# Two graph layers on one core: complex products added up in PSUM in the first batch, block sums of graph 56 and the order of graph 63

## Chip, cores, metric

One Trainium2 chip, one of its cores. The metric is the device time of one execution in microseconds (us); the time of a kernel is the median of its runs. The engines are called PE (TensorE), DVE (VectorE), ACT (ScalarE), POOL (GpSimd) and SP (SyncE, which here only issues transfers).

## What is computed

Input are 64 graphs of N = 256 nodes with D = 256 features, `x` (64, 256, 256), and their adjacency matrices `adj` (64, 256, 256), all in float32. Two layers follow each other; BN is a batch normalisation with given statistics, LN a normalisation over the features without weights.

```
# layer 0
h      = relu(BN1(conv1x1(x)))                       # over the nodes, D channels
x_conv = relu(BN2(conv17(h)) + x)
s      = x @ w_se.T + b_se                           # 3 features
A      = exp(-|s_i - s_j|^2) * adj
msg    = relu(x @ w_msg.T + b_msg)
x_nmp  = A @ msg
x1     = LN(x + GRUcell([x_conv, x_nmp], x))         # gates r, z, n
# layer 1
h      = LN(x1) * gamma + beta
conv   = (adj @ h) @ W_rel + b_rel + h @ W_root
out    = LN(x1 + (x1 + relu(conv)))
```

## The kernel before

**Batches.** The graphs are worked in 8 batches of 8. The convolution with 17 taps is computed for a whole batch in a transform domain: the features of the batch are folded and split by a tree of DVE steps over slots of one large tile, `XF` (also seen as `X`, with 256 columns to a slot), into 15 leaves, most of them complex pairs. Each complex leaf is multiplied by its filter with three real products, k1 = (sum slot) x w0, re x w1 and im x w2. `products` (L387) takes two leaves at a time: it writes the three products into three PSUM banks by `product` (L384, matmuls at L385), and its inner function `take` copies k1 to SBUF on ACT (L400) and writes k1 - p3 (DVE, L401) and k1 + p2 (DVE, L402) back into the slots. Seven such pairs and `last_products` make up the 15 leaves. The merges of the way back are DVE steps at L303 and L305 (each on the real and imaginary slots together), then `stt` (L104). At the end `second` and `third` write the slots that PE transposes back and adds to the transposed x (`turned_x`, L539, and L574, tile `ps_xc`); ACT takes the result through a relu into `xc` (L579).

**The first batch.** The convolution of batch 0 runs alone, ahead of the loop, with filters that are made on the way and lie in one tile (`w2all`, in the pool `first_pool`). Between its pairs of leaves (counted in `count`) stand steps for the first graphs: messages of graph 0 after the third pair and of graph 1 after the fourth (`messages`, L639, on PE, ACT and POOL), then factors and distances of graph 0, and after the leaf products messages of graph 2. `first_pool.close()` then lets `adj`, `wih` and `x` be loaded into the space.

**The loop.** For every graph the loop of a batch issues the gates of the GRU cell (`gates_rz`, L713 and L715, and `gates_n`, L725 and L727), the step `update` (new x and h), the transposes of h and the projection of the graph before (L869, L882), its aggregation (L894, tile `y`), and the message passing of graphs ahead. `pump` inserts steps of the next batch's convolution between them. `STAGE` says how far a convolution is; `pump` reads it to start preparations for the last batch.

**The last batch.** Graphs 56 to 62 compute their gates with seven block products in place of eight (`block_gates`, L774, tiles `ps_a` to `ps_d`, matmuls at L786, DVE's `onto` at L791). The left factors are blocks of x, nmp and xc and four sums of such blocks, which `block_sums(k, i)` makes with four DVE steps per input (L768 to L771). The second pair of products, in ps_b and ps_c, reads the sums of all three inputs. Graph 56's sums are made by `pump` in the loop of batch 6, once its inputs exist (`early_sums`, L1148); those of 57 to 62 are made in the turn of the graph before.

**The last graph.** `last_graph` (L919) works graph 63 in two halves of 128 nodes. `half(n)` is a generator with steps that the body calls by `step`: nn with a tanh; w, its statistics and POOL's power chain `scales` (L932, L933); h (L957) and the shift (POOL, L938 and L939); x1 (ACT, L960). Around them stand, in the order written out by hand, the gates, `project(62)`, `aggregate(62)`, the transposes of h (`turn_half`, L966) and the projections (`project_half`, L974) of each half, the sums over the neighbours (L1003) and the last normalisation. For n = 0 that is a shift on POOL and an activation on ACT (L1015), for n = 1 a DVE step (L1017); each half has its own output transfer.

**What sets the order.** Every engine runs its instructions in program order and waits at the first that isn't ready. PSUM has eight banks of one tag, handed out in turn by `bank`; a bank is reused when the readers of its last content are through.

Of the kernel before, what the change touches and what calls it, by code (L numbers as in the profile page):

```python
# [13 lines left out]
AF = mybir.ActivationFunctionType  # L14
ALU = mybir.AluOpType

P = 128
B, N, D = 64, 256, 256
C = D // P
# [10 lines left out]
BG = 8  # L30
NB = B // BG
# [16 lines left out]
LEAVES = [(V + k, V + 8 + k, a) for k, a in enumerate(leaf_angles(PI / 2, 8))]  # L48
# [28 lines left out]
def gnn_two_layers(  # L77
# [17 lines left out]
    nc = tc.nc  # L95
# [4 lines left out]
    def bank(name):  # L100
        return psum.tile([P, 512], F32, tag="ps", name=name)
# [143 lines left out]
    def sl(a, n, step=1):  # L245
        return X[:, a:a + n] if step == 1 else X[:, a:a + (n - 1) * step + 1:step]
# [133 lines left out]
        nc.sync.dma_start(out=t[:, :n], in_=w2m[first:first + n].rearrange("f c p o -> p f c o"))  # L380
        return lambda m, c: t[:, m, c, :]

    def product(ps, slot, w, m):
        for c in range(C):  # L384
            nc.tensor.matmul(ps, X[:, slot, c * P:(c + 1) * P], w(m, c), start=(c == 0), stop=(c == C - 1))  # L385

    def products(b, first, sums):  # L387

        p1, p2, p3 = bank("ps_k1"), bank("ps_k2"), bank("ps_k3")
        re, im, _ = LEAVES[first]  # L390
        for k in range(2):
            w = load_w(b, 3 * (first + k), 3)
            at = slice(k * D, (k + 1) * D)
            product(p1[:, at], sums + k, w, 0)
            product(p2[:, at], re + k, w, 1)
            product(p3[:, at], im + k, w, 2)

        def take():
            k1 = sl(sums, 2).rearrange("p s e -> p (s e)")
            nc.scalar.copy(k1, p1)  # L400
            nc.vector.tensor_sub(sl(re, 2).rearrange("p s e -> p (s e)"), k1, p3)  # L401
            nc.vector.tensor_add(sl(im, 2).rearrange("p s e -> p (s e)"), k1, p2)  # L402
        return take

    def last_products(b):
# [29 lines left out]
    def conv(b):  # L435
# [150 lines left out]
            yield from second(j)  # L586
        for j in range(8):
            yield from third(j)
        STAGE[b] = "out"

        def channels(q):
            for o in range(C):
# [128 lines left out]
    def gates_n(k, n):  # L721
        q, ins = inputs(k, n)
        pn = bank("ps_n")
        for c in range(C):
            nc.tensor.matmul(pn[:, D:], XT[k][:, c, q], whh[:, c, 2 * D:], start=(c == 0), stop=(c == C - 1))  # L725
        for i, t in enumerate(ins):
            nc.tensor.matmul(pn[:, :D], t, wih[:, i, 2 * D:], start=(i == 0), stop=(i == 3))  # L727
        nc.vector.tensor_add(RZ[k][1][:, n, :], pn, brzn[:, 2 * D:])  # L728
# [186 lines left out]
    def step(g):  # L915
        if g is not None:
            next(g, None)


    def last_graph(y_before, k):  # L920
        nn, w, y = (work.tile([P, C, D], F32, tag=t, name=t, bufs=b) for t, b in (("nn", 1), ("w", 1), ("y", 2)))
        H[k] = work.tile([P, C, D], F32, tag="h", name="h", bufs=1)
        X1[k] = work.tile([P, C, D], F32, tag="x1", name="x1", bufs=2)

        hT, hr = (XF[:, i * C * D:(i + 1) * C * D].rearrange("p (c n) -> p c n", c=C) for i in range(2))
        outs = []

        def scales(mv, columns):

            q = work.tile([P, 2], F32, tag="q", name="qh", bufs=4)  # L930
            for i, (f, e) in enumerate(columns):
                nc.gpsimd.tensor_scalar(q[:, i:i + 1], mv[:, 1:2], f, e, ALU.mult, ALU.add)  # L932
            nc.gpsimd.tensor_tensor(q[:, :len(columns)], q[:, :len(columns)], mhalf[:, :len(columns)], ALU.pow)  # L933
            return q

        def shift(mv, q):
            sh = work.tile([P, 1], F32, tag="sh", name="shh", bufs=4)
            nc.gpsimd.tensor_mul(sh, mv[:, 0:1], q[:, 0:1])  # L938
            nc.gpsimd.tensor_scalar(sh, sh, -1.0, None, ALU.mult)  # L939
            return sh  # L940

        def half(n):
            rz, gn = RZ[k]
            a, c = nn[:, n, :], w[:, n, :]
            stt(a, rz[:, n, :D], 1.0, gn[:, n, D:], op0=ALU.add, op1=ALU.mult)
            stt(a, a, 0.5, gn[:, n, :D])
            nc.scalar.activation(a, a, AF.Tanh)
            yield
            nc.vector.tensor_sub(c, XG[k][:, n, :], a)
            stt(c, rz[:, n, D:], 3.0, c, op0=ALU.add, op1=ALU.mult)  # L950
            stt(c, a, 4.0, c)
            mv = work.tile([P, 1, 2], F32, tag="mv", name="mvh", bufs=4)
            stats(mv, 0, c)
            mv = mv[:, 0, :]
            q = scales(mv, [(1.0, 4 * EPS), (1 + EPS, 4 * EPS * EPS)])
            yield
            nc.vector.tensor_scalar(H[k][:, n, :], c, mv[:, 0:1], q[:, 1:2], ALU.subtract, ALU.mult)  # L957
            sh = shift(mv, q)
            yield
            nc.scalar.activation(X1[k][:, n, :], c, AF.Identity, bias=sh, scale=q[:, 0:1])  # L960
            yield

        def turn_half(n):
            ps = bank("ps_hT")
            for c in range(C):
                nc.tensor.transpose(ps[:, c * P:(c + 1) * P], H[k][:, n, c * P:(c + 1) * P], ident)  # L966
            for c in range(C):
                nc.scalar.activation(hT[:, c, n * P:(n + 1) * P], ps[:, c * P:(c + 1) * P], AF.Identity,
                                     bias=gb[:, 1, c:c + 1], scale=gb[:, 0, c:c + 1])

        def project_half(n):
            ps = bank("ps_out")
            for c in range(C):
                nc.tensor.matmul(ps, hT[:, c, n * P:(n + 1) * P], wrr[:, c, :], start=(c == 0), stop=(c == C - 1))  # L974
            nc.scalar.copy(hr[:, n, :], ps[:, :D])
            outs.append(ps)

        halves_ = [half(n) for n in range(C)]
        gates_rz(k, 0)
        gates_n(k, 0)  # L980
        step(y_before)
        transposes_h(k - 1)
        step(halves_[0])
        gates_rz(k, 1)
        step(halves_[0])
        gates_n(k, 1)
        step(halves_[1])
        step(halves_[0])
        step(halves_[0])
        project(k - 1)  # L990
        step(halves_[1])
        turn_half(0)
        step(halves_[1])
        agg = aggregate(k - 1)
        step(agg)
        turn_half(1)
        step(halves_[1])
        project_half(0)
        project_half(1)
        step(agg)  # L1000
        for m in range(C):
            for n in range(C):
                nc.tensor.matmul(outs[n][:, D:], ADJ[k][:, m, n * P:(n + 1) * P], hr[:, m, :], start=False,  # L1003
                                 stop=(m == C - 1), skip_group_check=True)
        step(agg)
        for n in range(C):
            o = y[:, n, :]
            nc.vector.tensor_add(o, outs[n][:, D:], brel)
            stt(o, o, 0.0, X1[k][:, n, :], op0=ALU.max, op1=ALU.add)
            mv = work.tile([P, 1, 2], F32, tag="mv3", name="mvy", bufs=4)  # L1010
            stats(mv, 0, o)
            q = scales(mv[:, 0, :], [(1.0, EPS / 4)])
            if n == 0:
                sh = shift(mv[:, 0, :], q)
                nc.scalar.activation(o, o, AF.Identity, bias=sh, scale=q[:, 0:1])  # L1015
            else:
                nc.vector.tensor_scalar(o, o, mv[:, 0, 0:1], q[:, 0:1], ALU.subtract, ALU.mult)  # L1017
            (nc.sync, nc.scalar)[n].dma_start(out=out[k, n * P:(n + 1) * P, :], in_=o)


# [78 lines left out]
    while STAGE.get(0) != "inverse":  # L1099
        if next(first) is None:  # L1100
            count += 1
            if count == 3:
                messages(0, True)
            elif count == 4:
                messages(1, True)
            elif count == 5:
                factors(0)
            elif count == 6:
                distances(0)
    messages(2, True)  # L1110
    first_pool.close()

# [16 lines left out]
    POINTS = 10  # L1129
    y_left = None  # L1130
    sums_left = weight_blocks()
    early_sums = [0, 1, 2]
    for b in range(NB):
        coming = conv(b + 1) if b + 1 < NB else iter(())
        done, at, goal = 0.0, 0, BG * POINTS - 6
# [1 line left out]
        def pump():  # L1137
            nonlocal done, at
            at += 1
            while done < CONV_WEIGHT * at / goal:  # L1140
                t = next(coming, 1e9)
                if t is None:
                    break
                done += t
            if STAGE.get(NB - 1) in ("inverse", "out"):
                next(sums_left, None)

            if STAGE.get(NB - 1) == "out" and (NB - 1) * BG in NMP and len(early_sums) > (done < 1e8):  # L1148
                block_sums((NB - 1) * BG, early_sums.pop(0))

        if b == NB - 1:
            break
# [44 lines left out]
    for _ in sums_left:  # L1197
        pass
    first_k = (NB - 1) * BG
    for i in early_sums:  # L1200
        block_sums(first_k, i)
    for k in range(first_k, B - 1):
        load(k + 3)
# [74 lines left out]
```

## Time and profile before

| what | us |
|---|---|
| median of five runs | 2257.08 |
| lowest, highest | 2253.61, 2258.67 |
| profiled execution | 2253.61 |
| its span, first to last instruction | 2251.8 |
| TensorE's granted clock, mean over the span | 0.998 |

In the lines that follow, L12 is line 12 of the kernel before. PE is a matmul, PEld its weight load, SPq, ACTq and the like an engine's queue. A line of the chain of waits has its start, its length, engine, output tile, line and how many instructions. A line of the timeline has start, length, engine, line, operation, output and inputs, shape, and in brackets the idle time of the engine just before it with what ended it. A line of the windows has for each engine the busy time and number of instructions, then the granted clock of TensorE (1.00 is full), the busy share of the transfer engines and GB/s.

### The profile page before, as it was taken

How to read it: one execution, taken by the hardware profiler on the slowest of the kernel's cores; microseconds unless marked ns; L12 is line 12 of the kernel's file. 1: busy time of each engine (PE TensorE's matmuls, PEld its weight loads, DVE VectorE, ACT ScalarE, POOL GpSimd, SP SyncE). 2: the span in 40 equal slices, each digit the busy share in tenths (PEclk: the TensorE clock that was granted, in tenths of full speed). 3: DMA queues.
4: the chain of work that ended last, by engine and by line, in shares of the span. 5: the costliest groups of instructions: out<-in, count | busy, mean ns of one | idle time of the engine just before them, and what ended most of it. 6: DMA issues, size and time to landing. Idle time of an engine off the chain costs nothing.

```text
span 2251.8 us, 24641 instructions
## 1 busy us (share of the span) xinstructions
PE 2206.0 (98%) x8400; PEld 1463.6 (65%) x8400; DVE 1720.8 (76%) x3329; ACT 767.0 (34%) x1587; POOL 471.5 (21%) x933
## 2 busy tenths in 40 slices
PE   8999999999999999999999999999999999999998
PEld 5775666667666666656766566665666666666665
DVE  6976889388892988749987498865979478896675
ACT  6433223432235322443224432244222432224333
POOL 0101212221221221213212231221212222212212
PEclk9999999999999999999999999999999999999999
DMA  5932432214423143231522334222332314321110
GB/s 148 317 108 69 137 108 93 98 48 140 136 75 103 38 151 120 75 106 65 167 75 75 103 110 140 82 81 79 131 122 75 113 52 140 116 84 49 42 33 20
DMA packets 212682, 226.69 MB, mean 101 GB/s; under 512 B 22103, under 2 KB 203854, under 8 KB 212558
## 3 DMA queue, kind: packets, MB, share of 16 engines
q1 hardware_dynamic: 190128, 191.27, 26.4%
q10 hardware_dynamic: 22430, 33.86, 4.3%
q8 instruction: 67, 1.10, 0.2%
q14 instruction: 57, 0.47, 0.1%
HBM read 179.22 MB, written 45.88 MB: 100 GB/s over the span
## 4 chain that ended last, share of the span: by engine, by line
PE 80%; DVE 15%; issue 2%; POOL 1%; DMA 1%; ACT 1%; ACTq 0%; SPq 0%; POOLq 0%; DVEq 0%
PE ps_rz L715 16%; PE ps_k L385 10%; PE ps_rz L713 8%; PE ps_n L727 8%; PE ps_out L882 7%; DVE XF L104 5%; PE ps_c L466 5%; PE ps_nmp L697 5%; PE ps_msg L647 4%; PE ps_out L894 4%; PE ps_n L725 4%; DVE w L104 1%; DVE XF L362 1%; PE ps_dist L685 1%; DVE bst L824 1%
## 5 line engine op out<-in xcount | busy, mean ns | idle before, releaser
L104 DVE SCALAR_TENSOR_TENSOR XF<-XF 128x512 f32<-128x512 f32 (+2 forms) x800 | 507.7, 665 | 7.4
L846 POOL TENSOR_SCALAR q<-mv 128x2 f32<-128x2 f32 x63 | 31.9, 506 | 1441.1 <-DVE mv L825 1441.1
L385 PE MATMUL ps_k<-w,XF 128*128 128x256 f32 x1316 | 298.3, 382 | 14.2 <-ACT AT L687 11.6
L385 PEld LDWEIGHTS ps_k<-w,XF 128*128 128x128 f32 x1316 | 246.8, 190 | 60.6 <-ACT AT L687 17.3
L728 DVE TENSOR_TENSOR gn<-ps_n,brzn 128x512 f32<-128x512 f32 x114 | 78.3, 687 | 197.7 <-PE ps_n L727 197.7
L719 ACT ACTIVATE rz<-rz 128x512 f32<-128x512 f32 x114 | 71.8, 630 | 462.4 <-DVE rz L718 462.4
L882 PE MATMUL ps_out<-wrr,hT 128*128 128x512 f32 x504 | 226.6, 592 | 0.0
L713 PE MATMUL ps_rz<-whh,xT 128*128 128x512 f32 x456 | 214.6, 593 | 0.0
L715 PE MATMUL ps_rz<-wih,nmp 128*128 128x512 f32 x456 | 214.4, 592 | 0.0
L715 PE MATMUL ps_rz<-wih,xc 128*128 128x512 f32 x456 | 214.4, 592 | 0.0
L718 DVE TENSOR_TENSOR rz<-ps_rz,brzn 128x512 f32<-128x512 f32 x114 | 77.7, 681 | 153.4 <-PE ps_rz L715 153.3
L882 PEld LDWEIGHTS ps_out<-wrr,hT 128*128 128x128 f32 x504 | 96.0, 190 | 96.0 <-issue 84.3
L715 PEld LDWEIGHTS ps_rz<-wih,xc 128*128 128x128 f32 x456 | 86.9, 190 | 108.8 <-issue 108.6
L715 PEld LDWEIGHTS ps_rz<-wih,nmp 128*128 128x128 f32 x456 | 86.9, 190 | 108.8 <-issue 108.8
L658 ACT ACTIVATE msg<-msg 128x512 f32<-128x512 f32 x61 | 38.4, 630 | 337.9 <-DVE msg L656 337.9
L647 PE MATMUL ps_msg<-wms,xT 128*128 128x260 f32 x512 | 132.1, 396 | 4.9 <-DVE XF L401 4.9
L362 DVE TENSOR_TENSOR XF<-XF 128x512 f32<-128x512 f32 (+3 forms) x128 | 125.4, 1004 | 1.7
L466 PE MATMUL ps_c<-xTc,w 128*128 128x512 f32 x256 | 116.1, 597 | 7.0 <-ACT xTc L458 7.0
L697 PE MATMUL ps_nmp<-AT,msg 128*128 128x256 f32 x512 | 121.1, 380 | 0.0
L713 PEld LDWEIGHTS ps_rz<-whh,xT 128*128 128x128 f32 x456 | 82.3, 191 | 57.6 <-issue 54.4
L894 PE MATMUL ps_out<-hr,adj 128*128 128x256 f32 x504 | 119.6, 380 | 0.0
L883 ACT COPY hr<-ps_out 128x256 f32<-128x256 f32 x126 | 46.7, 372 | 211.1 <-PE ps_out L882 211.1
(197 smaller groups left out, 3790.0 us busy)
## 6 DMA issues: line engine op xcount, KB each, us to landing
w<-w2m SPq DMA_DIRECT2D x105, 768.0 KB, 5.9
xn<-in_x_dram SPq DMA_DIRECT2D x32, 512.0 KB, 4.4
xt<-xTc ACTq DMA_DIRECT2D x32, 512.0 KB, 3.2
xT<-xt SPq DMA_DIRECT2D x64, 256.0 KB, 2.9
xb<-in_x_dram SPq DMA_DIRECT2D x32, 512.0 KB, 5.8
adj<-in_adjT_dram SPq DMA_DIRECT2D x64, 256.0 KB, 2.7
x<-in_x_dram SPq DMA_DIRECT2D x64, 256.0 KB, 3.0
out_dram<-y ACTq DMA_DIRECT2D x63, 256.0 KB, 2.2
```

Of the source, the lines that this page charges most:

```text
L104: nc.vector.scalar_tensor_tensor(o, in0, s, in1, op0=op0, op1=op1)
L362: (nc.vector.tensor_add if add else nc.vector.tensor_sub)(sl(o, n), sl(a, n), sl(b, n))
L385: nc.tensor.matmul(ps, X[:, slot, c * P:(c + 1) * P], w(m, c), start=(c == 0), stop=(c == C - 1))
L466: nc.tensor.matmul(pss[o], w1[:, c, o * P:(o + 1) * P], xTc[:, c, :], start=(c == 0), stop=(c == C - 1))
L647: nc.tensor.matmul(ps[:, :D + 4], XT[k][:, c, m * P:(m + 1) * P], wms[:, c, :], start=(c == 0), stop=(c == C - 1 and not idle))
L697: nc.tensor.matmul(ps[:, d * N:(d + 1) * N], MSG[k][:, m, d * P:(d + 1) * P], AT[k][:, m, :], start=(m == 0), stop=(m == C - 1))
L713: nc.tensor.matmul(prz, XT[k][:, c, q], whh[:, c, 0:2 * D], start=(c == 0), stop=False)
L715: nc.tensor.matmul(prz, t, wih[:, i, 0:2 * D], start=False, stop=(i == 3))
L725: nc.tensor.matmul(pn[:, D:], XT[k][:, c, q], whh[:, c, 2 * D:], start=(c == 0), stop=(c == C - 1))
L727: nc.tensor.matmul(pn[:, :D], t, wih[:, i, 2 * D:], start=(i == 0), stop=(i == 3))
L882: nc.tensor.matmul(ps, hT[:, c, n * P:(n + 1) * P], wrr[:, c, :], start=(c == 0), stop=(c == C - 1))
L894: nc.tensor.matmul(po, ADJ[k][:, m, n * P:(n + 1) * P], hr[:, m, :], start=False, stop=(m == C - 1), skip_group_check=True)
```

## The change

Five things are changed.

- In batch 0, `products_added` takes the place of `products`. It uses two banks for a pair. PE first writes k1 into the first bank, ACT copies it to the sum slot; then PE writes im x w2 into the second bank and adds re x w1 onto k1 in the first. `take` copies that sum to the imaginary slots on ACT, and DVE has only the subtraction left.
- The messages of graph 1 move from behind the fourth pair of leaves to behind all leaf products, just ahead of those of graph 2.
- The sums of graph 56 are made at the head of the last batch and no longer in the loop of batch 6; the mark "out" goes.
- In graph 63, statistics and h of a half become one step (a `yield` goes), and the steps, transposes, projections and the aggregation stand in another order.
- The last normalisation of half 1 is done as that of half 0, by POOL and ACT.

```diff
-    def product(ps, slot, w, m):
+    def product(ps, slot, w, m, first=True):
         for c in range(C):
-            nc.tensor.matmul(ps, X[:, slot, c * P:(c + 1) * P], w(m, c), start=(c == 0), stop=(c == C - 1))
+            nc.tensor.matmul(ps, X[:, slot, c * P:(c + 1) * P], w(m, c), start=first and c == 0, stop=(c == C - 1),
+                             skip_group_check=True)
...
     def products(b, first, sums):
+        if b == 0:
+            return products_added(first, sums)
...
+    def products_added(first, sums):
+        p1, p3 = bank("ps_k1"), bank("ps_k3")
+        re, im, _ = LEAVES[first]
+        w = [load_w(0, 3 * (first + k), 3) for k in range(2)]
+        at = [slice(k * D, (k + 1) * D) for k in range(2)]
+        k1 = sl(sums, 2).rearrange("p s e -> p (s e)")
+        for k in range(2):
+            product(p1[:, at[k]], sums + k, w[k], 0, k == 0)
+        nc.scalar.copy(k1, p1)
+        for k in range(2):
+            product(p3[:, at[k]], im + k, w[k], 2)
+        for k in range(2):
+            product(p1[:, at[k]], re + k, w[k], 1, False)
+        def take():
+            nc.scalar.copy(sl(im, 2).rearrange("p s e -> p (s e)"), p1)
+            nc.vector.tensor_sub(sl(re, 2).rearrange("p s e -> p (s e)"), k1, p3)
+        return take
...
-        STAGE[b] = "out"
...
             q = scales(mv, [(1.0, 4 * EPS), (1 + EPS, 4 * EPS * EPS)])
-            yield
             nc.vector.tensor_scalar(H[k][:, n, :], c, mv[:, 0:1], q[:, 1:2], ALU.subtract, ALU.mult)
             sh = shift(mv, q)
             yield
...
         step(halves_[0])
+        step(halves_[0])
         gates_n(k, 1)
         step(halves_[1])
-        step(halves_[0])
-        step(halves_[0])
+        turn_half(0)
         project(k - 1)
+        project_half(0)
         step(halves_[1])
-        turn_half(0)
-        step(halves_[1])
+        turn_half(1)
         agg = aggregate(k - 1)
         step(agg)
-        turn_half(1)
+        project_half(1)
         step(halves_[1])
-        project_half(0)
-        project_half(1)
         step(agg)
...
             q = scales(mv[:, 0, :], [(1.0, EPS / 4)])
-            if n == 0:
-                sh = shift(mv[:, 0, :], q)
-                nc.scalar.activation(o, o, AF.Identity, bias=sh, scale=q[:, 0:1])
-            else:
-                nc.vector.tensor_scalar(o, o, mv[:, 0, 0:1], q[:, 0:1], ALU.subtract, ALU.mult)
+            sh = shift(mv[:, 0, :], q)
+            nc.scalar.activation(o, o, AF.Identity, bias=sh, scale=q[:, 0:1])
...
-            elif count == 4:
-                messages(1, True)
...
+    messages(1, True)
     messages(2, True)
     first_pool.close()
...
-    early_sums = [0, 1, 2]
...
-            if STAGE.get(NB - 1) in ("inverse", "out"):
+            if STAGE.get(NB - 1) == "inverse":
                 next(sums_left, None)
-            if STAGE.get(NB - 1) == "out" and (NB - 1) * BG in NMP and len(early_sums) > (done < 1e8):
-                block_sums((NB - 1) * BG, early_sums.pop(0))
...
-    for i in early_sums:
+    for i in range(3):
         block_sums(first_k, i)
```

## The prediction

> **What bounds the kernel now.** The first page view, busy time by engine, and the fourth, the chain that ended last, say that TensorE is the bound for most of the span:
>
> ```profile
> PE 2206.0 (98%) x8400; PEld 1463.6 (65%) x8400; DVE 1720.8 (76%) x3329; ACT 767.0 (34%) x1587; POOL 471.5 (21%) x933
> PE 80%; DVE 15%; issue 2%; POOL 1%; DMA 1%; ACT 1%; ACTq 0%; SPq 0%; POOLq 0%; DVEq 0%
> ```
>
> The 15% on DVE decide this case, because the change sits at the places where PE stops leading. There are three: the first batch (DVE leads from 105 us on), the gates of graph 56, and graph 63. I read the chain in each, then the timeline with its releasers. First the chain around the first batch (start, us, what):
>
> ```profile
> 100.14 5.39 PE ps_k L385 x24
> ...
> 105.63 0.69 DVE XF L401
> 106.31 0.61 DVE XF L402
> ...
> 106.94 0.70 DVE XF L303
> ...
> 144.75 5.24 PE ps_xc L574 x30
> 149.99 1.79 PE ps_xc L539 x16
> 151.78 3.57 PE ps_xc L574 x32
> ```
>
> DVE takes the chain over from PE at the fourth pair and gives it back 39 us later at L574. Its sub, add and merges run without a gap. 30 records of L574 first cost 5.24 us and then 32 cost 3.57. The timeline and the windows (sums, TensorE clock, DMA share) say why:
>
> ```profile
> 144.15 5.84 PE L574 MATMUL ps_xc<-ident,XF 128*128 128x128 f32 x32 [3.41 <-DVE XF L104]
> ...
> 146.00:147.00 1.00, 1.00 (x6) 1.00 (x6) 0.97 (x3) 1.00 (x2) 0.00 (x0) 0.50 0.10 33
> 149.00:150.00 1.00, 1.00 (x11) 1.00 (x11) 1.00 (x3) 0.87 (x2) 0.00 (x0) 1.00 0.00 0
> ```
>
> PE idled 3.41 us for DVE, and then worked at clock 0.50 until about 149. Now the end of the span: the chain through the gates of graph 56, and lines of the timeline there and in graph 63.
>
> ```profile
> 2054.15 1.72 PE ps_d L786 x6
> 2055.87 1.72 PE ps_b L786 x6
> 2057.59 1.72 PE ps_c L786 x6
> ```
> ```profile
> 2057.99 0.53 DVE L791 TENSOR_TENSOR XF<-ps_a,brzn 128x384 f32<-128x384 f32 x1
> ...
> 2232.49 0.18 DVE L825 BATCH_NORM_AGGREGATE mvh<-bst 128x2 f32<-128x6 f32 x1
> 2232.64 0.69 DVE L728 TENSOR_TENSOR gn<-ps_n,brzn 128x512 f32<-128x512 f32 x1
> ...
> 2238.20 0.41 DVE L957 TENSOR_SCALAR h<-w,mvh,qh 128x256 f32<-128x256 f32 x1 [1.37 <-POOL qh L933]
> ...
> 2248.55 0.41 DVE L1017 TENSOR_SCALAR y<-y,mvy,qh 128x256 f32<-128x256 f32 x1 [1.30 <-POOL qh L933]
> ```
>
> PE runs through the gates without a gap (each piece begins where the last ended). In graph 63 an h waits for POOL's power chain, and the last DVE step too.
>
> **First batch: products added in PSUM.** Per pair, one DVE add (L402) goes and one 128x512 ACT copy comes; TensorE runs the same matmuls, the four of "re" now second into the first bank. On DVE, sub to merge takes 106.94 - 105.63 = 1.31 us now. Without the add the merge follows the sub directly, 0.72 (as L303 to L305 stand now), so 0.59 per pair. Pairs 1 to 3 give nothing: DVE waits for PE at the fourth anyway (idle 103.4 to 105.63). Pairs 4 to 7 give 4 x 0.59 = 2.36. The ACT copy (group mean 579 ns) has to end before the merge as well: PE ends at 105.53, ACT can be done near 106.2, the merge is due at 106.35; for pairs 5 to 7 PE is many us ahead of DVE. The added wait on PE, that the second use of the bank comes after ACT's copy of k1, is covered: the copy ends 0.83 after its four matmuls, PE has the 1.73 us of "im" to run first, 0.9 us to spare. Without that cover it would be 0.83 a pair on the four pairs that PE leads, 3.3 us.
>
> Graph 1's messages (4 x 260-wide matmuls and two short ones per half, 3.31 us of PE at 105.35) move behind the leaf products. PE's total up to the end of nmp at 140.73 stays, so PE is free at the same time. Behind them now stand messages of graph 2 and the transposes; their banks come free by DVE subs that end 3 us or more before PE gets there. Their four ACT copies and five POOL steps move to idle engines. The pool of the first filters closes 3.3 us earlier, so SP issues adj, wih and x earlier (129.86 now); its order is the same.
>
> DVE's gate of L574 moves from 144.15 to 141.79, PE's idle from 3.41 to 1.06. At 2.64 us of idle before the transposes of h at 204.31 the clock stayed 1.00, so it should stay full here. Then PE is gated by DVE's four last stages, each 2.6 us; the last slot is ready at 152.65 - 2.36 = 150.29, and 14 of its 16 records of 0.112 follow: end near 152.0 in place of 155.35. The gain is **3.3**; 2.36 if the clock falls all the same; 0 if something else ends that stretch; at most 3.9 if the stages themselves gain half a microsecond.
>
> **Block sums of graph 56.** Twelve DVE steps leave the loop of batch 6 (2039.9 to 2048.6, in gaps where DVE waits for PE or ACT; nothing gets faster there, since nn at 2048.42 waits for ACT). They now come after the statistics of y, just ahead of L791 at 2057.99. One set runs 0.94, three 2.77. The third product (ps_b) needs the first sum of all three sets; the last of these is ready at 2057.99 + 2 x 0.94 + 0.26 = 2060.13, its last two matmuls (0.70 with the latency) end at 2060.83, where they ended at 2057.59. That is **3.24** on PE, and no gap up to 2188 takes it up. PE's idle of 2.45 in one piece stays under the 2.64 that kept the clock. Bounds: 2.4 if only the idle counts, 3.9 if the clock drops for 1.5 us.
>
> The Trainium skill, "Perfetto Trace Analysis", section "Identifying the Most-Contended Engine", says to judge TensorE's headroom by its weight loads, not by matmul time. By that, 65% here leaves a third free, the stall could be made up, and the sum below would be near -0.8 and not +2.4. The chain shows back-to-back matmuls after this point; I go by the chain.
>
> **Graph 63.** With the yield gone, DVE issues h of half 0 right after its statistics and waits for POOL's power. For half 1 that is 2238.20 - 2236.65 = 1.55. So h(0) starts at 2232.49 + 1.55 = 2234.04 and is done where PE can begin its transposes at 2234.51; PE ended its last product at 2232.44, and the transposes now stand ahead of the 3.4 us of project(62): 2.07 idle. Queued behind the waiting DVE step are gn of half 1 (2232.64 to 2234.37, +1.73), and through it nn on ACT and h(1): 2239.93, transposes 2240.40. In their place PE has project(62), 3.43, and half 0's projection, 1.72, to 2240.1: 0.3 idle. aggregate(62) and half 1's projection, 1.72 each, end at 2244.3, where the projections ended at 2242.54: **+1.75**. y of graph 62 is through DVE before the last sums come. The last normalisation takes POOL's two steps (0.19 and 0.23 with their gaps 0.54) and 0.60 on ACT for 0.41 on DVE: **+0.75**. Together 2.5; if PE finds the half's idle covered, as the order may intend, 0.75 and at best 0; if 2.07 and 0.3 idle both count, 3.1.
>
> **Sum.** -3.3 + 3.24 + 2.5 = +2.4 us. The profiled execution took 2253.61 (span 2251.8 and 1.8 around it), the lowest of five; its sum gives 2256.0, and on the median 2257.08 it is **2259.5**. That is 0.11%; about 0.2%, 4.5 us, is what a measurement of this kernel can tell from no change.
>
> **Rivals.** First, slower: the first batch's gain doesn't reach PE. Place: the merge L303 takes real and imaginary slots in one instruction, so it waits for the later of DVE's sub and ACT's copy, and ACT's copies of k1 and im stand in one queue with the messages' copies. From 0.6 us of lateness per pair the whole saving is gone: +3.24 + 2.5 = +5.7, 2262.8. For it: at pair 4 ACT has only 0.15 us to spare; against it: ACT is a third busy and PE leads by many us from pair 5. Halved clocks after the new idles of 2.45 and 2.07 would lead to the same side, some 1.5 more each.
>
> Second, near no change or faster: the sums are taken up, or the tail's new order hides its stall. -3.3 + 3.24 + 0.75 = +0.7, or with both -3.3 + 0 + 0.75 = -2.5, 2254.6. For it, PE has other work in graph 63 (project(62)); against it, that work is queued behind the waiting transposes.
>
> Third, that the change doesn't do what it says: seven adds are absent from the new program order and ACT copies are there, so only the place of the gain is open, which is the first rival.
>
> **Chances.** Main case 55%, the first rival 30%, the second 15%. The likeliest time is 2259.5, the main case with its bounds 2258 to 2262; the first rival with noise reaches 2264, the second 2255, and the range of 2255.5 to 2263.5 leaves a tenth at each end. Over +4.5: a fifth of the main case and three quarters of the first rival, 34%. Under -4.5: a quarter of the second at most, 4%. Within: 62%.
>
> **What would show it.** Right: DVE reaches L574's gate near 141.8, the windows there keep 1.00, L574 ends near 152; PE idles about 2.5 ahead of ps_b in graph 56 and 2 ahead of the first half's transposes in graph 63; POOL's L938 and L939 stand between the last power and the last ACT step, and the span ends near 2254.2. Wrong: merges that wait for ACT, a PE wait inside the leaf products, a clock of 0.50 at the gates of graph 56, or no PE gap there.

## The result and the profile after

The changed kernel takes 2261.44 us (median), the kernel before in all its runs 2256.11. The ratio is 1.0023, with a 95% interval of 1.0017 to 1.0028: slower by 5.2 us (3.8 to 6.3). The forecast was +2.4 us, with 2259.5 in a range of 2255.5 to 2263.5. The sign and the range hold, the size is half of what came, and the likeliest class, within 0.2%, was just missed. That 2259.5 lies as near as it does is in part luck: it starts from the median of five runs, 2257.08, which all 46 runs put 1.0 us lower. The profiled execution took 2260.49, its span is 2258.7.

All five parts can be found in the trace where the prediction put them. First the page's busy time and its chain by engine.

```profile
PE 2211.0 (98%) x8400; PEld 1465.4 (65%) x8400; DVE 1716.9 (76%) x3321; ACT 771.6 (34%) x1595; POOL 468.6 (21%) x935
PE 78%; DVE 14%; DMA 3%; issue 2%; POOL 1%; ACT 1%; SPq 0%; ACTq 0%; POOLq 0%; DVEq 0%
```

DVE has 3.9 us less, ACT 4.6 more. The chain through the first batch (start, length, what):

```profile
99.27 10.56 PE ps_k L386 x48
...
127.54 7.46 DMA bhh<-in_rows_dram
...
141.88 5.24 PE ps_xc L598 x30
147.13 1.79 PE ps_xc L563 x16
148.91 3.57 PE ps_xc L598 x32
```

DVE no longer carries 39 us without a break: PE runs pair after pair, and further down the loads that follow the pool's closing appear. DVE comes back into the chain after them. But the first 30 transposes cost 5.24 us, as before. The timeline has the wait ahead of them, and the windows (busy time of PE, PEld, DVE, ACT, POOL, then TensorE's clock) the reason.

```profile
104.75 0.69 DVE L426 TENSOR_TENSOR XF<-XF,ps_k 128x512 f32<-128x512 f32 x1 [3.52 <-PE ps_k L386]
105.55 0.69 DVE L303 TENSOR_TENSOR XF<-XF 128x512 f32<-128x512 f32 x1
...
141.28 5.84 PE L598 MATMUL ps_xc<-ident,XF 128*128 128x128 f32 x32 [1.61 <-DVE XF L104]
```
```profile
142.00:142.50 0.50, 0.50 (x5) 0.50 (x6) 0.47 (x2) 0.00 (x0) 0.00 (x0) 1.00 0.08 27
142.50:146.00 3.50, 3.50 (x19) 3.50 (x19) 3.40 (x6) 2.12 (x4) 0.00 (x0) 0.51 0.00 1
146.00:146.50 0.50, 0.50 (x6) 0.50 (x6) 0.50 (x2) 0.23 (x1) 0.00 (x0) 1.00 0.00 0
```

The wait fell from 3.41 to 1.61 us, and the clock was halved all the same, for 3.4 us. The gates of graph 56, in the timeline:

```profile
2052.15 0.60 PE L809 MATMUL ps_a<-whh,xT 128*128 128x256 f32 x2
...
2057.88 0.26 DVE L791 TENSOR_TENSOR XF<-xT 128x128 f32<-128x128 f32 x1
...
2058.29 0.67 PE L809 MATMUL ps_b<-wsum,XF 128*128 128x256 f32 x2 [2.53 <-DVE XF L791]
...
2059.15 1.85 PE L809 MATMUL ps_b<-wsum,XF 128*128 128x384 f32 x4 [0.19 <-DVE XF L791]
...
2060.83 1.88 PE L809 MATMUL ps_c<-wsum,XF 128*128 128x256 f32 x6
...
2062.55 0.60 PE L892 MATMUL ps_hT<-ident,h 128*128 128x128 f32 x4
```

The kernel before has, in the same place and at the last group of ps_n in graph 63:

```profile
2052.26 0.60 PE L786 MATMUL ps_a<-whh,xT 128*128 128x256 f32 x2
...
2059.15 0.60 PE L869 MATMUL ps_hT<-ident,h 128*128 128x128 f32 x4
...
2231.58 1.03 PE L727 MATMUL ps_n<-wih,nmp 128*128 128x256 f32 x4
```

DVE starts the sums where `onto` (L791 of the kernel before) started, and PE waits 2.53 + 0.19 us for them. From the start of ps_a to that of ps_hT it takes 10.40 us (2052.15 to 2062.55), before 6.89 (2052.26 to 2059.15): +3.5. Nothing of it is made up in the 172 us that follow: from ps_a to the last group of ps_n it is 182.83 (to 2234.98, next view) and was 179.32. And graph 63:

```profile
2234.98 1.03 PE L750 MATMUL ps_n<-wih,nmp 128*128 128x256 f32 x4
...
2235.89 0.18 DVE L848 BATCH_NORM_AGGREGATE mvh<-bst 128x2 f32<-128x6 f32 x1
...
2237.44 0.41 DVE L979 TENSOR_SCALAR h<-w,mvh,qh 128x256 f32<-128x256 f32 x1 [1.36 <-POOL qh L956]
...
2237.76 0.68 DVE L751 TENSOR_TENSOR gn<-ps_n,brzn 128x512 f32<-128x512 f32 x1
...
2237.99 0.41 PE L988 MATMUL ps_hT<-ident,h 128*128 128x128 f32 x2 [1.99 <-DVE h L979]
...
2238.24 5.30 PE L905 MATMUL ps_out<-wrr,hT 128*128 128x512 f32 x8
...
2255.25 0.60 ACT L1034 ACTIVATE y<-y,shh,qh 128x256 f32<-128x256 f32 x1 [0.94 <-POOL shh L962]
```

h of half 0 waits 1.55 us behind its statistics, gn of half 1 is 1.87 behind those statistics where it was 0.15, and PE idles 1.99 ahead of the transposes. project(62), which took 3.60, takes 5.30: the clock again. From the end of the last group of ps_n (0.86 after its start) to the end of the span it was 19.4 us (2251.8 - 2232.44) and is 22.9 (2258.7 - 2235.84): +3.5.

### The profile page after: what moved, and what is told of

It reads as the page before. It is cut to its first block, busy times and chain, and to the rows that moved or that the text cites. A ratio compares the mean times of both kernels' runs of the same rounds, so it can differ in the third digit from the quotient of the medians.

```text
span 2258.7 us, 24649 instructions
## 1 busy us (share of the span) xinstructions
PE 2211.0 (98%) x8400; PEld 1465.4 (65%) x8400; DVE 1716.9 (76%) x3321; ACT 771.6 (34%) x1595; POOL 468.6 (21%) x935
## 4 chain that ended last, share of the span: by engine, by line
PE 78%; DVE 14%; DMA 3%; issue 2%; POOL 1%; ACT 1%; SPq 0%; ACTq 0%; POOLq 0%; DVEq 0%
PE ps_rz L738 14%; PE ps_k L386 11%; PE ps_rz L736 7%; PE ps_n L750 7%; PE ps_out L905 7%; PE ps_c L490 5%; PE ps_nmp L720 5%; DVE XF L104 4%; PE ps_msg L670 4%; PE ps_out L917 4%; PE ps_n L748 4%; DMA w<-w2m 2%; PE ps_w L230 2%; DVE w L104 2%; DVE bst L847 1%
## 5 line engine op out<-in xcount | busy, mean ns | idle before, releaser
L738 PE MATMUL ps_rz<-wih,xc 128*128 128x512 f32 x456 | 214.3, 592 | 0.0
L738 PE MATMUL ps_rz<-wih,nmp 128*128 128x512 f32 x456 | 214.3, 592 | 0.0
L738 PEld LDWEIGHTS ps_rz<-wih,nmp 128*128 128x128 f32 x456 | 86.8, 190 | 108.9 <-issue 108.9
L738 PEld LDWEIGHTS ps_rz<-wih,xc 128*128 128x128 f32 x456 | 86.9, 190 | 108.8 <-issue 108.6
```

What stands on the lines that cost most here:

```text
L738: nc.tensor.matmul(prz, t, wih[:, i, 0:2 * D], start=False, stop=(i == 3))
```

## The experiments

Each is the kernel before with the edit named, and its lines have its own numbers. Times are ratios to the kernel before, turned into us on 2256; of a kernel that ran once only the trace is read.

**The first batch alone, with and without the move of the messages.** The edit is the change's own `products_added`; the second kernel leaves out

```diff
-            elif count == 4:
-                messages(1, True)
...
+    messages(1, True)
     messages(2, True)
```

> The kernel before with the first batch's part of the change alone (products added in PSUM, messages of graph 1 behind the leaf products). Theory A, that the parts of the change add up and this one is a gain that the others outweigh: DVE reaches the gate of the first transposes about 2.0 us earlier than before, counted from the fourth pair of leaves; the time falls by 2.0 if TensorE still works at half clock after its wait there, by 3.3 if it doesn't. Rival B, that nothing of this gain reaches the end: no change, 0 +- 0.5.

> The kernel before with the products added in PSUM, but the messages of graph 1 where they were, behind the fourth pair. Theory A (the adds taken from DVE carry the gain): as the run with the messages moved, within 0.5 us, -2.0 to -3.3. Rival C (the move of the messages carries it, since the later pairs come to TensorE 3.3 us earlier): no gain, 0 +- 0.5.

Measured: 0.9999 (0.9991 to 1.0008), -0.2 us (-2.0 to +1.8), and 0.9997 (0.9988 to 1.0005), -0.7 (-2.7 to +1.1). The times alone can't decide between a gain of 2 and none. The traces can. The measure is from the end of the fourth pair on PE to the distances of graph 1, in kernels whose clock stayed full or fell at the transposes; the chain of the kernel with the messages left in place reads

```profile
101.32 5.38 PE ps_k L386 x24
...
148.30 1.79 PE ps_xc L563 x16
150.08 3.57 PE ps_xc L598 x32
153.66 0.63 PE ps_dist L709 x4
```

which is 153.66 - 106.70 = 46.96, at full clock. The old products at full clock (so in the trace of graph 63 alone, below) need 49.03. With a drop (the clock at half during the transposes) it is 47.8 for the new products in two traces, and 49.6 to 50.6 for the old ones in six. So up to the distances the part gains 1.9 to 2.1 us at full clock, 1.8 to 2.8 where it falls in both. Where the messages stand makes 0.1 at equal clock (47.1 with the messages moved, in the two kernels with the wait filled, below): the adds carry the gain, theory A. Whether all of it reaches the end is not shown: from there to graph 56 the twelve traces need 1896 to 1904 us, with 0 to 5 clock drops, and a difference of 1 or 2 us is lost in that.

**The sums of graph 56 alone.**

```diff
-        STAGE[b] = "out"
...
-    for i in early_sums:
+    for i in range(3):
         block_sums(first_k, i)
```

> The kernel before with the sums of graph 56 made at the head of the last batch, and nothing else changed. Theory A: TensorE waits about 2.5 us ahead of ps_b in graph 56 and the time rises by 3.2 to 3.5, as the trace of the whole change shows between ps_a and ps_c. Rival D, that the stall is made up later: 0 to 1.

Measured: 1.0011 (1.0001 to 1.0021), +2.5 us (0.2 to 4.7). The trace has the wait, and a drop behind it that the whole change's profile did not have:

```profile
2060.22 0.70 PE L785 MATMUL ps_b<-wsum,XF 128*128 128x256 f32 x2 [2.54 <-DVE XF L767]
2061.09 2.93 PE L785 MATMUL ps_b<-wsum,XF 128*128 128x384 f32 x4 [0.16 <-DVE XF L767]
2063.81 2.06 PE L785 MATMUL ps_c<-wsum,XF 128*128 128x256 f32 x6
```

Four matmuls of ps_b took 2.93 us in place of 1.85. From ps_a to ps_hT it is 11.62, +4.7. From ps_a to the last group of ps_n it is 4.7 longer too, while the ten traces with the old sums agree there to 0.02 us. The stall stays, against rival D; it is 3.5 without and 4.7 with a drop.

**Graph 63 alone, and its two halves.** The third kernel keeps the `yield` and takes the new order, the fourth takes out the `yield` and keeps PE's order:

```diff
         step(halves_[0])
+        turn_half(0)
         project(k - 1)
+        project_half(0)
```
```diff
             q = scales(mv, [(1.0, 4 * EPS), (1 + EPS, 4 * EPS * EPS)])
-            yield
             nc.vector.tensor_scalar(H[k][:, n, :], c, mv[:, 0:1], q[:, 1:2], ALU.subtract, ALU.mult)
```

> The kernel before with the new order of graph 63 and its last normalisation, and nothing else changed. Theory A: TensorE waits 2.0 us for h of half 0; the time rises by 2.3 where the clock stays full after that wait, and by 3.4 where it falls to half for 3.4 us. Rival E, that the order alone is neutral and only the last normalisation costs: +0.5 to +0.8.

> The kernel before with the new order of graph 63, but statistics and h of a half stay two steps (the yield stays) and the last normalisation stays on DVE. From the end of ps_n to the end of the span it was 19.4 us before and 22.9 with the whole change. Theory A: the stall of TensorE comes from the place of the transposes ahead of project(62), so it idles 2.2 us for h of half 0 here too, but half 1 is no longer held up on DVE: 19.4 + 0.3 to 1.0, and up to 1.7 more if the clock falls. Rival H, that the order alone costs the whole: 21.5 or more at full clock.

> The kernel before with statistics and h of a half in one step (the yield gone), the order of PE's work as before and the last normalisation on DVE. Theory A: no stall for half 0, which project(62) hides, but gn of half 1 waits behind h of half 0 for 1.7 us on DVE, and TensorE waits 2.3 in place of 0.6 for h of half 1: 19.4 + 1.7 = 21.1 from the end of ps_n to the end of the span. Rival H: 19.4, the yield is neutral.

The whole of graph 63: 1.0012 (1.0001 to 1.0022), +2.7 us (0.2 to 5.0). From the end of ps_n to the end of the span its trace has 2262.3 - 2239.42 = 22.9, with the drop. The seven traces with the old graph 63 agree on this length to 0.02, so single traces can be read. The order alone has 2255.4 - 2234.83 = 20.6 at full clock (+1.2, above the 0.3 to 1.0 that theory A gave and below the rival's 21.5), the yield alone 2256.8 - 2235.70 = 21.1 (+1.7, as theory A said).

```profile
2237.18 0.41 PE L966 MATMUL ps_hT<-ident,h 128*128 128x128 f32 x2 [2.19 <-DVE h L957]
2237.43 3.60 PE L882 MATMUL ps_out<-wrr,hT 128*128 128x512 f32 x8
```
```profile
2240.54 2.00 PE L894 MATMUL ps_out<-hr,adj 128*128 128x256 f32 x8 [1.03 <-ACT hr L883]
...
2243.64 0.44 PE L965 MATMUL ps_hT<-ident,h 128*128 128x128 f32 x2 [1.10 <-DVE h L956]
```

In the first of them (the order alone) PE waits 2.19 ahead of half 0, and project(62) keeps its 3.60. In the second (the yield alone) half 0 is hidden, and half 1 is paid for by two waits of 1.03 and 1.10. Each half of the edit costs by itself; neither is neutral. The whole of graph 63 at full clock stands in no trace.

**When does the clock fall?** The reference row of the prediction was a wait of 2.64 at 204 us after which the clock stayed full. The same wait stands in every kernel here, and in five of the twelve traces the clock did fall behind it. First the row of the kernel before, then those of the kernel whose wait in the first batch is filled (below):

```profile
204.31 0.78 PE L869 MATMUL ps_hT<-ident,h 128*128 128x128 f32 x4 [2.64 <-DVE h L856]
```
```profile
200.65 1.14 PE L894 MATMUL ps_hT<-ident,h 128*128 128x128 f32 x4 [2.64 <-DVE h L881]
201.58 3.15 PE L738 MATMUL ps_rz<-whh,xT 128*128 128x512 f32 x4
```

The four matmuls of L738 take 3.15 us there; they take 1.88 at full clock. To measure the rule by itself, 70 bursts with waits between them were put behind the kernel:

```diff
+    for i in range(70):
+        ps = bank("ps_n")
+        for _ in range(22):
+            nc.tensor.matmul(ps, z[:, :P], wrr[:, 0, :], start=True, stop=True)
+        steps = i % 5
...
+        stt(z, ps, 0.0, wrr[:, 0, :])
```

> The kernel before, followed by 70 bursts of 22 matmuls (128x512) with a wait between them that a chain of 1 to 5 DVE steps makes: stalls of about 1, 1.7, 2.4, 3.1 and 3.8 us, 14 of each, at all kinds of places in time. Its time is longer by the bursts and isn't compared. Theory F: the clock is judged once in a fixed period (the drops in the traces so far begin and end 3.41 us apart), so a stall of 1 never halves the clock, one over 3.4 always, and one of 1.7 to 3.1 in a part of the cases that grows with its length; the price of a drop is 1.7 us of TensorE's time. Rival G: there is a fixed length between 2.64 and 3.41 from which each stall halves the clock, and the drops after shorter stalls have another cause: the 1.7 and 2.4 never, the 3.8 always.

| wait before a burst, us | waits | clock fell |
|---|---|---|
| 0.78 | 14 | 0 |
| 1.51 (one 1.60) | 14 | 0 |
| 2.23 (one 2.33) | 14 | 2 |
| 2.96 (one 3.05) | 14 | 14 |
| 3.69 | 13 | 13 |

One of the two at 2.23, beside one of 1.51 without a drop, in the timeline, and the windows behind the first:

```profile
2427.45 3.55 PE L1240 MATMUL ps_n<-wrr,XF 128*128 128x512 f32 x5 [2.24 <-DVE XF L104]
...
2518.09 19.15 PE L1240 MATMUL ps_n<-wrr,XF 128*128 128x512 f32 x44 [1.51 <-DVE XF L104]
```
```profile
2427.45:2428.50 1.05, 1.05 (x3) 0.57 (x4) 0.00 (x0) 0.00 (x0) 0.00 (x0) 1.00 0.00 0
2428.50:2432.00 3.50, 3.50 (x6) 1.46 (x5) 0.00 (x0) 0.00 (x0) 0.00 (x0) 0.51 0.00 0
```

The clock fell 1.1 us after the wait was over, and for 3.41 us. Wherever a drop begins while PE works, it begins on one grid: 2339.85 and 3783.69, for example, are 1443.84 = 423.0 times 3.4133 us apart. The two waits of 2.23 that were followed by a drop lie wholly inside one period of that grid; of one that wasn't, 2537.24 to 2539.47, the grid's line at 2537.82 cuts off 0.58. All 69 waits sort by the longest piece that lies inside one period: up to 1.95 us there was no drop (40 waits), from 2.19 on always one (29).

The same count explains the reference row. In the kernel before, a drop begins at 145.26, and 17 periods later, at 203.29, the grid cuts the wait of 2.64 into 1.62 and 1.02: no drop. In the trace with the wait filled the whole wait lies inside the period that ends at 200.70, where the clock falls. In the twelve traces the longest piece of this wait was 1.37 to 2.01 in the seven without a drop, and 2.06 to 2.64 in the five with one. Even a wait of 3.41 passed once, in the trace of graph 63 alone, where the grid cut it into 1.98 and 1.43:

```profile
144.52 2.43 PE L574 MATMUL ps_xc<-ident,XF 128*128 128x128 f32 x16 [3.41 <-DVE XF L104]
```

All this fits theory F, that the clock is judged once in a period. What it expected at 1.5 (some drops) and at 3 (some waits without one) did not come between the bursts; the 70 waits fell on few phases of the grid, so their shares are no probabilities. The rival's fixed length above 2.64 fails by the two drops at 2.23.

**Waits filled.** Two kernels put idle matmuls into waits: seven into the first batch's (with the change's products), and two behind the distances of graphs 5, 13 to 53, where PE waits 1.12 us after short matmuls. A third takes both, with four in the first batch.

```diff
+    def fill():
+        for _ in range(7):
+            nc.tensor.matmul(LAST_ST[0][:, N:], ident, XT[2][:, 0, :], start=True, stop=True)
...
+        if k % BG == 5 and k < (NB - 1) * BG:
+            for m in range(C):
+                nc.tensor.matmul(pss[m][:, N:], ident, XT[k][:, 0, :], start=True, stop=True)
```

> The kernel before with the first batch's part of the change, and seven idle matmuls (128x256, result unused) in TensorE's wait between nmp and the first transposes with x_conv. Theory F: with the wait of 1.6 filled, the clock stays full at the transposes in every execution: from the end of the fourth pair to the distances of graph 1 it takes 47.0, as where the clock stayed full by chance, and not 47.85. The time falls by 0.5 to 1 against the same kernel without them, -2 to -3 against before. Rival: the idle matmuls only push the transposes back, and nothing is gained.

> The kernel before with two idle matmuls (128x256, results unused) behind the distances of graphs 5, 13, ... 53, where TensorE does four short matmuls (4x256), some products and then waits 1.1 us for ACT. In ten traces of this study the clock fell to half in 15 of these 70 places. Theory F, that a drop is charged at its period for the work done in it, and costs up to 1.7 us: the idle matmuls stay inside the wait (0.9 of 1.1 us), no drop is left at these places, the mean granted clock rises by about 0.001 and the time falls by 1.5 to 2.5. Rival G (only long single waits halve the clock): no change, or up to 1 slower where the idle matmuls push the products back.

> The kernel before with the first batch's part of the change, four idle matmuls in its wait and the two of the run above behind the distances; no sums and no order of graph 63 changed. Theory A and F together: 2.0 from the first batch and 1.5 to 2.5 from clock drops that no longer happen, -3.5 to -4.5 against before, the fastest version of this study. Rival: the first batch gives nothing in time, -1.5 to -2.5.

Measured: 0.9993 (0.9983 to 1.0003), -1.6 us (-3.8 to +0.7); 0.9999 (0.9990 to 1.0008), -0.2 (-2.3 to +1.8); 0.9985 (0.9976 to 0.9993), -3.4 (-5.4 to -1.6). With the first batch filled, the transposes run at full clock and end 47.1 after the fourth pair; the seven matmuls take 3.0 us, twice the wait, and cost 0.1, because DVE's last stages set the end. Behind the distances, the two traces show no drop in 14 places (15 of 70 before, so none in 14 would come by chance one time in thirty), and the mean clock of the runs is 0.9979 and 0.9983, that of the kernel before beside them 0.9969. The first kernel's interval holds both no change and the -2 to -3 that was expected. The second kernel's time does not show the gain of 1.5 to 2.5 that was expected; its interval just reaches it, so what these drops cost stays open. The third kernel, 2252.27 us beside 2255.91, is the only one whose interval lies wholly below the kernel before; its interval takes in the expected -3.5 to -4.5. The first two kernels gave -1.6 and -0.2, so how the gain divides stays open too.

## Why the prediction was right and where it was off

**First batch: the term of -3.3 was -2.0.** Two steps of it were mis-sized. From sub to merge it is 0.79 (104.75 to 105.55, and the same in the later pairs) and not 0.72, so a pair gives 0.52 and not 0.59 (why this step takes longer behind the sub was not tried); DVE's gate comes 2.0 earlier (36.5 for 38.5 us from the fourth sub) and not 2.36. The larger error is the clock: "so it should stay full here" rested on one row with a wait of 2.64, and that row was chance: the grid happened to cut the wait in two. After a wait of 1.61, wholly inside one period, it fell. Taken at equal clock, the part is worth what DVE gains, not more. The merge did not wait for ACT and the move of the messages cost nothing, as was said. So the first rival, whose +5.7 is nearer to the result than the main case, had its main mechanism wrong; what it named in passing, a halved clock behind the new waits, came behind the wait in graph 63.

**Block sums: +3.24 was +3.5.** The mechanism, the place of the wait and its size (2.45 forecast, 2.53 found, and 0.19 after it) are right. That the idle "stays under the 2.64 that kept the clock" was no ground. In the profile of the whole change the grid cut the 2.53 into 1.64 and 0.89, without a drop; in that of the sums alone the 2.54 lay inside one period and the drop came. The bound of 3.9 that was given for it was too low by 0.8.

**Graph 63: +2.5 was +3.5.** h(0) at 1.55 behind its statistics, the 1.99 of idle (2.07 forecast) and gn's delay stand in the trace as worked out, and the yield alone costs 1.7. What the sum left out, and only the first rival named, is the drop: project(62) is 1.7 longer. With it the last sums start 3.0 later, once the 3.40 by which this trace is behind at ps_n is taken off (2242.38 before; 2248.75 - 3.40 = 2245.35 now), where 1.75 was forecast. The last normalisation cost 0.5 (from the first DVE step on the last sums to the last output issue 5.28 for 4.76), not 0.75.

**The sum.** -2.0 + 3.5 + 3.5 = +5.0, for +5.2 (3.8 to 6.3) measured; the parts alone give -0.2, +2.5 and +2.7 with intervals of two us on each side. The drops differ from execution to execution, so that the parts of two profiles come so near the difference of the medians is in part chance. The forecast's +2.4 misses 1.3 in the first batch, 0.3 in the sums and 1.0 in graph 63. The two profiled spans differ by 6.9, more than the parts: the rest lies in the loop, in events such as a drop after a wait of 1.12 us at 1914, which the other trace doesn't have:

```profile
1913.66 0.89 PE L386 MATMUL ps_k<-w,XF 128*128 128x256 f32 x2 [1.12 <-ACT AT L710]
```

**The rules.** The Trainium skill, "Perfetto Trace Analysis", "Identifying the Most-Contended Engine", judges TensorE's headroom by MFU (the share of peak arithmetic) and by the busy share of its weight loads. The 65% of the latter, read as room, misled here: the stall of graph 56 was not made up, 3.51 us longer from ps_a to the last ps_n. On the clock, the skill's "TensorE: Matmul & The Clock Gate", Part 1, says that activity is watched in a free-running window of 3413 ns; the 423.0 periods above agree. The same page, in "HAM oscillation — how this bites in real kernels", gives the abstract rule "no PE-idle gaps >~3.4µs". The traces are stricter: the clock fell after waits of 1.12, 1.61, 1.99 and 2.23 us, and the measurement decides.

## What to carry to other kernels

A stall of the engine that sets the end costs its length and, from one to three us on, the chance of a clock drop behind it of up to 1.7 us; price it as such, and compare two versions only with the same clock drops. One row in which a wait did no harm is a sample, not a rule; look for the same wait in other executions first. A step that another engine's chain waits for belongs where its own engine idles, even if it stands there in another stage of the program.

## What the runs showed of the hardware

The granted clock falls on a fixed grid of 3.4133 us that runs through an execution (in the changed kernel's trace the drops in the first batch and in graph 63 begin at 142.5 and 2238.3, 614 periods apart), and a drop mostly lasts one period. It falls behind a wait of which enough lies inside one period: between dense 128x512 bursts up to 1.95 us was harmless and 2.19 was not, at the wait of 2.64 in graph 0 up to 2.01 was and 2.06 was not. Where the grid lies differs between executions, and so the same wait is followed by a drop in five of twelve traces. That short matmuls on few rows and transposes count for less than dense ones would fit the drops after 1.12 and 1.61 us, beside none after 1.51 between dense bursts; this was argued and not tried by itself.
